# First layer of a two-layer metaformer: all eight images' scan blocks in one stream, the router as one stage behind them

## The chip, the cores and the metric

The kernel runs on one core of a Trainium2 chip. The metric is the device time of one execution in microseconds: 20141.26 us, the median of three runs (20123.66 to 20142.09). A core has five instruction queues that run in order and wait for each other through semaphores: PE (TensorE, matrix products into PSUM), DVE (VectorE), ACT (ScalarE), POOL (GpSimd) and SP (SyncE, which here issues the DMA transfers). Work is kept in order on each queue by the program; a queue whose first instruction waits holds everything behind it.

## The reference, cut to what matters

The net has two layers on an input of 8 images, 128 channels, 64 x 64 points (L = 4096). Only the first layer's mixer and the router of its mixture of experts are touched by the change.

```python
# layer 0, mixer: x = x + L0_conv(ln_c(x))
x_seq = x.reshape(b, c, L).swapaxes(1, 2); skip = x_seq
x_norm = (x_seq - mu) * rsqrt(var + 1e-5) * ln_g + ln_b
xp = x_norm @ in_w.T
x_tb = xp.reshape(b, h, w, D).swapaxes(1, 2).reshape(b, L, D)
U = stack([xp, flip(xp, 1), x_tb, flip(x_tb, 1)], 0)      # four directions
Y = vmap(_mamba)(U, ...)
...
out = skip_gate * (y_fused @ out_w.T) + (1.0 - skip_gate) * skip

def _mamba(u, ...):
    xh, z = split(u @ in_w.T, 2)
    xh = silu(conv1d(xh) + conv_b)                        # 4 taps
    dt, Bm, Cm = split(xh @ xproj_w.T, [R, R + N])        # N = 16 states
    dt = softplus(dt @ dt_w.T + dt_b)
    # h = exp(dt*A) * h + dt*x*B ;  y = sum_n h*C, along 4096 positions
    y = _selective_scan(xh, dt, A, Bm, Cm) + xh * Dp      # Dp is the "D term"
    return (y * silu(z)) @ out_w.T

# layer 0, experts: t = t + L0_ffn(ln_t(t))
probs = softmax(x @ gate_w.T + gate_b, axis=1)            # over the 4096 tokens, 64 experts
topv, topi = top_k of each expert, K = 8
pooled = einsum('bked,bke->bed', gathered tokens, topv)   # then the experts, then a scatter
```

## The kernel before, in words

Tensors lie as 128 channels on the partitions and positions along the free axis. `S` = 512 is a slice (8 slices an image), `CH` = 1024 a chunk of the scan; an image has 4 directions `d` of 4 chunks `j`, 16 chunks.

**A chunk's scan** works on 16 *slots*. 128 channels x 16 states are 2048 recurrences; a slot takes 128 of them (8 channels x 16 states). In slot n, in `scan_blocks`: PE spreads dt over the states into a PSUM tile `dA` (6 products in bf16, `expand`); ACT takes its exp; SP broadcasts 8 rows of `dtx_d` from DRAM to 128 partitions (`xE`, L621, 512 KB, four buffers); POOL multiplies it with B (`bx`, three buffers); DVE does the scan (L627) and the product with C (`hc`, L335), and keeps the last column (`last`, L347). PE then sums the states of four slots into the tile `y` by 8 products with `collect`. The code issues `xE` three slots ahead and `dA` and `bx` one slot ahead. On every engine the order is the order of the code: `ordered` ties each instruction to the one before it.

**A chunk's other steps** are put into slots by hand, in a table in `scan_steps`: each entry is a slot relative to the chunk's first. Slots -18 to -2, which lie in the chunk before, prepare the chunk: the four taps of the conv folded into `W_taps`, silu by tanh, dt by softplus, `dtx` (POOL, then a store to DRAM by SP, L526), B and C spread over the states, dt split into three bf16 parts. Slots 12 to 20 finish it: z product and its silu (`zs`), `skip` (DVE, L344: y + D x), `gate_y` (POOL: times zs, two halves), `out_product` (PE) and `out_add` (DVE: adds into `r`, the image's residual). ACT loads the tables of exp and ln at slot -11 and of exp and tanh at slot -4.

**Between two images** `run` closes the scan's pools and runs two generators in turns: `route_tokens` of the image just done and `scan_inputs` of the next. `route_tokens` stores `r` to `x1` in DRAM, takes the layer norm of each slice, the logits of 64 experts (on 64 partitions), turns the tokens over (`tk`), and then does the softmax over 4096 tokens, the eight largest (`MAX8`, `MATCH_REPLACE8`), and the pooled tokens (32 turns of P, 32 products). `scan_inputs` loads x, takes two norms one after the other (the outer `ln_c` and the mixer's own), projects into `xp`, copies the turned image `xt`, and writes `(1 - skip) x_norm + x` into `r`. After the last image only the router runs; then come the experts.

PSUM holds 8 banks: two `dA` tiles of two banks, `y` of two, and two banks `m`, which all other products of the scan stage share in turn.

Of the kernel before, what the change touches and what calls it, by code (L numbers as in the profile page):

```python
# [131 lines left out]
def layout(inputs):  # L132
# [46 lines left out]
    a.add("gate_b", i["L0_ffn_gate_b"])  # L179
# [99 lines left out]
class Net:  # L279
# [111 lines left out]
    def scan_weights(self, pool):  # L391
# [45 lines left out]
        self.wname, self.wt = "first", first  # L437

    def scan_steps(self, ch, xp, r, pl, ps):
# [76 lines left out]
        def dt(q):  # L516
            p = v[f"d{q}"]
            self.tt(p, v[f"sp_u{q}"], p, ALU.subtract)
            self.tt(make(f"dt{q}", 2), v[f"sp_r{q}"], p, ALU.add)
# [27 lines left out]
        def skip():  # L547
            self.stt(make("yt", 1, CH), ch["xs"], self.w(f"D{d}"), ch["y"], ALU.mult, ALU.add)

        def gate_y(q):  # L550
            yt = v["yt"][:, half[q]]
            self.tt(yt, yt, v["zs"][:, half[q]], ALU.mult, pool)

        def out_product(q):
            self.mm(bank(f"o{q}"), self.Wo[:, d, :], v["yt"][:, half[q]])

        def out_add(q):
            p, lo = v[f"o{q}"], CH * j + q * S
            lo = L - S - lo if back else lo
            if d < 2:  # L560
                to = r[:, lo : lo + S]
                to = to[:, ::-1] if back else to
            else:
                w0 = lo // 64
                to = r.rearrange("p (h w) -> p w h", w=64)[:, w0 : w0 + S // 64, :]
                to = to[:, ::-1, ::-1] if back else to
                p = p.rearrange("p (w h) -> p w h", h=64)
            self.tt(to, to, p, ALU.add)
# [10 lines left out]
            (-4, self.table, EXP_TANH_SET), (-3, part, 1, 1), (-3, rest, 1, 0), (-2, rest, 1, 1),  # L579
            (12, z_product, 0), (13, z_product, 1), (13, z_gate, 0), (14, z_gate, 1),  # L580
            (15, gated, v, "zs", 0), (16, gated, v, "zs", 1),
            (17, skip), (18, gate_y, 0), (19, gate_y, 1), (19, out_product, 0), (20, out_product, 1),
            (19, out_add, 0), (20, out_add, 1),
# [3 lines left out]
    def scan_blocks(self, xp, xt, r, pl, ps):  # L587
# [5 lines left out]
        chunks = [{"d": d, "j": j} for d in range(4) for j in range(NCH)]  # L593
        todo = {}
        for i, ch in enumerate(chunks):
            for at, step, *args in self.scan_steps(ch, xp if ch["d"] < 2 else xt, r, pl, ps):
                todo.setdefault(NQ * i + at, []).append((step, args))
# [5 lines left out]
        for n in range(min(todo), max(todo) + 1):  # L603
# [31 lines left out]
            if n % 4 < 2 and 4 <= n < total + 4:  # L635
# [4 lines left out]
                for g in range(4):  # L640
                    self.mm(ch["y"][32 * g : 32 * g + 32, h * S : (h + 1) * S], self.k("collect")[:, 32 * k : 32 * k + 32],
                            hcs[g0 + g][:, h * S : (h + 1) * S], start=k == 0, stop=k == 3)
# [5 lines left out]
        self.silus_done([])  # L648

# [7 lines left out]

    def scan_inputs(self, b, r, xp, xt, wk, ps):

        nc = self.nc  # L660
        made = [{} for _ in range(NS)]

        def bank(name):
            return ps.tile([C, S], F32, tag="b", bufs=4, name=name)

        def center(s):
            v = made[s]
            if s == 0:
                for t in (xp, xt):
                    nc.vector.memset(t[:, :PAD], 0.0)  # L670
                    nc.vector.memset(t[:, PAD + L :], 0.0)
            x = v["x"] = wk.tile([C, S], F32, name="x", bufs=4)
            nc.sync.dma_start(x, self.A["x"][b][:, s * S : (s + 1) * S])
            p = bank("ln_m")
            self.mm(p, self.k("mean"), x)
            v["xc"] = wk.tile([C, S], F32, name="xc", bufs=3)
            self.tt(v["xc"], x, p, ALU.subtract)
            v["sq"] = wk.tile([C, S], F32, name="xsq", bufs=3)
            self.act(v["sq"], v["xc"], AF.Square)

        def scales(s):
            v = made[s]
            p = bank("ln_v")
            self.mm(p, self.k("mean"), v["sq"])

            a, q = v["sq"], wk.tile([C, S], F32, name="xlq", bufs=3)
            self.act(a, p, AF.Ln, bias=self.k("e6"))
            self.act(q, a, AF.Exp, scale=-1.0)
            self.act(a, a, AF.Exp, scale=-0.5)
            self.tt(q, p, q, ALU.mult)  # L690
            self.tt(v["xc"], v["xc"], a, ALU.mult)
            self.stt(r[:, s * S : (s + 1) * S], v["xc"], self.unskip, v["x"], ALU.mult, ALU.add)
            v["q"] = q

        def second(s):
            v = made[s]
            self.rsqrt(v["q"], v["q"], self.k("e5"))
            self.tt(v["xc"], v["xc"], v["q"], ALU.mult, nc.gpsimd)
            self.ts(v["xc"], v["xc"], self.w("ln_g"), ALU.mult, self.w("ln_b"), ALU.add)

        def project(s):
            p = bank("xp_p")
            self.mm(p, self.w("in_w"), made[s]["xc"])
            xq = xp[:, PAD + s * S : PAD + (s + 1) * S]
            nc.scalar.copy(xq, p)
            nc.gpsimd.tensor_copy(
                xt[:, PAD : PAD + L].rearrange("p (w h) -> p h w", h=64)[:, s * 8 : s * 8 + 8, :],
                xq.rearrange("p (h w) -> p h w", w=64),
            )
            made[s] = None  # L710

        yield from self.pipeline(NS, (center, scales, second, project))

    def first_mixer(self, b, r, xp, xt):

        nc, tc = self.nc, self.tc
        with tc.tile_pool(name=f"scan{b}", bufs=1) as pl2, tc.tile_pool(name=f"scanps{b}", bufs=1, space=PSUM) as ps2:
            self.scan_blocks(xp, xt, r, pl2, ps2)

    def route_tokens(self, b, r, pl, wk, ps):  # L720

        nc = self.nc
        nblk = L // 128
        pr = pl.tile([NE, L], F32, name="pr")
        tk = pl.tile([128, nblk, C], F32, name="tk")
        ms = pl.tile([NE, NS], F32, name="ms")
        made = [{} for _ in range(NS)]

        def bank(name):
            return ps.tile([C, S], F32, tag="c", bufs=3, name=name)  # L730

        def center(s):
            v, sg = made[s], slice(s * S, (s + 1) * S)
            nc.sync.dma_start(self.x1[b][:, sg], r[:, sg])
            p = bank("ln_m")
            self.mm(p, self.k("mean"), r[:, sg])
            v["xc"] = wk.tile([C, S], F32, name="tn", bufs=3)
            self.tt(v["xc"], r[:, sg], p, ALU.subtract)
            v["sq"] = wk.tile([C, S], F32, name="tsq", bufs=3)
            self.act(v["sq"], v["xc"], AF.Square)  # L740

        def scale(s):
            v = made[s]
            p = bank("ln_v")
            self.mm(p, self.k("mean"), v["sq"])
            self.rsqrt(v["sq"], p, self.k("e5"))
            self.tt(v["xc"], v["xc"], v["sq"], ALU.mult)

        def logits(s):
            v, sg = made[s], slice(s * S, (s + 1) * S)  # L750
            p = bank("lg_p")
            self.mm(p[:NE], self.w("gate_w"), v["xc"])
            self.act(pr[:, sg], p[:NE], AF.Identity, bias=self.w("gate_b")[:NE])
            nc.vector.tensor_reduce(ms[:, s : s + 1], pr[:, sg], AX.X, ALU.max)
            p = bank("tp")
            for u in range(S // 128):
                nc.tensor.transpose(p[:, u * 128 : (u + 1) * 128], v["xc"][:, u * 128 : (u + 1) * 128], self.k("ident"))
            nc.scalar.copy(tk[:, s * 4 : s * 4 + 4, :].rearrange("p u c -> p (u c)"), p)
            made[s] = None

        yield from self.pipeline(NS, (center, scale, logits))
        m = pl.tile([NE, 1], F32, name="m")
        nc.vector.tensor_reduce(m, ms, AX.X, ALU.max)
        self.ts(m, m, -1.0, ALU.mult)
        sm = pl.tile([NE, 1], F32, name="sm")
        self.act(pr, pr, AF.Exp, bias=m, accum_out=sm)
        yield
        nc.vector.reciprocal(sm, sm)
        self.ts(pr, pr, sm, ALU.mult)
        m8 = pl.tile([NE, 8], F32, name="m8")  # L770
        nc.vector.max(m8, pr)
        yield
        P = pl.tile([NE, L], F32, name="P")
        nc.vector.match_replace(out=P, in_to_replace=m8, in_values=pr, imm_value=0.0)
        yield
        self.tt(P, pr, P, ALU.subtract)
        nc.sync.dma_start(self.P[b], P)
        yield
        pool = ps.tile([C, NE], F32, tag="pool", bufs=1, name="pool_p")
        PT = [None] * NS  # L780

        def turned(s):
            p = bank("Pt_p")
            for u in range(4):
# [897 lines left out]
    def run(self, ctx):  # L1682
# [13 lines left out]
        with tc.tile_pool(name="mid", bufs=1) as mp:  # L1696
            self.pooled = mp.tile([C, NE, nb], F32, name="pooled")
            with tc.tile_pool(name="l0", bufs=1) as pl:
# [3 lines left out]
                for b in range(nb + 1):  # L1702
                    with tc.tile_pool(name=f"in{b}", bufs=1) as rp, tc.tile_pool(name=f"inw{b}", bufs=2) as wk, \
                            tc.tile_pool(name=f"inps{b}", bufs=1, space=PSUM) as ps:
                        gens = []
                        if b:
                            gens.append(self.route_tokens(b - 1, r, rp, wk, ps))
# [43 lines left out]
```

## Time and profile before

| what | us |
|---|---|
| median of three runs | 20141.26 |
| the profiled execution, its own time | 20168.29 |
| its span, first to last instruction | 20166.5 |
| mean granted TensorE clock of the span | 0.942 of full speed |
| first scan starts | 130.5 |
| last scan ends | 9566.1 |
| spans of the eight images' scans, first start to last end | 1041.5, 1046.8, 1076.4, 1036.8, 1058.8, 1060.4, 1064.8, 1058.1 |
| last image's pooled tokens are copied, the experts begin | 9663.2 |

The rows of the profile read as follows. A group has the line of kernel.py, the engine, the operation, output <- input by tile names, shape, count, busy time and the mean length of one; behind it the idle time that the engine had just before, and what ended it. Many lines are those of helpers (L288 every matmul, L335 every tensor_tensor, L296 every activation), so a group is known by its tiles. A float32 matmul stands as two rows. In the first layer these are the instructions that the change and the prediction speak of:

| instruction | shape | count | mean us |
|---|---|---|---|
| scan, `dA<-dA,last,bx` (DVE, L627) | 128 x 1024 | 1536 | 2.350 |
| `hc<-dA,C` (DVE) | 128 x 1024 | 2048 | 1.224 |
| `bx<-xE,B` (POOL) | 128 x 1024 | 2048 | 2.354 |
| exp of `dA` (ACT) | 128 x 1024 | 2048 | 1.088 |
| skip, `yt<-xs,w_first,y` (DVE, L344) | 128 x 1024 | 128 | 1.272 |
| gate_y, `yt<-yt,zs` (POOL) | 128 x 512 | 256 | 1.268 |
| out_add, `r<-r,m` (DVE) | 128 x 512 | 256 | 0.675 to 1.305 |
| `MAX8`, `MATCH_REPLACE8`, `P<-pr,P` (DVE) | 64 x 4096 | 8 each | 4.42, 4.40, 4.42 |

### The profile page before, as it was taken

How to read it: one execution, taken by the hardware profiler on the slowest of the kernel's cores; microseconds unless marked ns; L12 is line 12 of the kernel's file. 1: busy time of each engine (PE TensorE's matmuls, PEld its weight loads, DVE VectorE, ACT ScalarE, POOL GpSimd, SP SyncE). 2: the span in 40 equal slices, each digit the busy share in tenths (PEclk: the TensorE clock that was granted, in tenths of full speed). 3: DMA queues.
4: the chain of work that ended last, by engine and by line, in shares of the span. 5: the costliest groups of instructions: out<-in, count | busy, mean ns of one | idle time of the engine just before them, and what ended most of it. 6: DMA issues, size and time to landing. Idle time of an engine off the chain costs nothing. (4 is left out here: it accounts for less than half of the span.)

```text
span 20166.5 us, 298179 instructions
## 1 busy us (share of the span) xinstructions
PE 16460.5 (82%) x113085; PEld 8450.3 (42%) x113085; DVE 15697.6 (78%) x20826; ACT 11182.7 (55%) x15819; POOL 9162.0 (45%) x6292
## 2 busy tenths in 40 slices
PE   6777777777777777777887889999999998998898
PEld 2222222222222222222644666666666666665343
DVE  7989899898998989899254677676767676776886
ACT  5555555555555555555253666666666666665553
POOL 6767677686767767577010222222222222221443
PEclk9989999899999999899686999999999999999899
DMA  4435354343544445444441001010001000001222
GB/s 115 139 109 136 108 133 133 110 140 107 135 116 125 136 109 133 107 138 127 134 129 53 27 27 28 26 28 26 28 26 28 26 28 26 27 27 32 81 99 78
DMA packets 814167, 1684.33 MB, mean 84 GB/s; under 512 B 180859, under 2 KB 413211, under 8 KB 803803
## 3 DMA queue, kind: packets, MB, share of 16 engines
q1 hardware_dynamic: 812734, 1665.25, 29.4%
q8 instruction: 896, 14.68, 0.3%
q14 instruction: 537, 4.40, 0.1%
HBM read 1440.67 MB, written 224.26 MB: 83 GB/s over the span
## 5 line engine op out<-in xcount | busy, mean ns | idle before, releaser
L335 POOL TENSOR_TENSOR bx<-xE,B 128x1024 f32<-128x1024 f32 x2048 | 4819.7, 2354 | 1471.4 <-DMA xE<-dtx_d 1347.8
L288 PE MATMUL dA<-parts,expand 128*128 128x512 bf16 x12288 | 3182.7, 397 | 2113.9 <-DVE last L347 1573.3
L296 ACT ACTIVATE dA<-dA,negA 128x1024 f32<-128x1024 f32 x2048 | 2228.6, 1088 | 3692.1 <-PE dA L288 3672.4
L627 DVE TENSOR_TENSOR_SCAN dA<-dA,last,bx 128x1024 f32<-128x1024 f32 x1536 | 3610.2, 2350 | 206.8 <-POOL bx L335 200.0
L288 PEld LDWEIGHTS <-expand 128*128 128x128 bf16 x12288 | 1072.0, 100 | 4822.3 <-DVE last L347 2751.8
L344 DVE SCALAR_TENSOR_TENSOR E_cm<-E_cm,gm_cm 128x1024 f32<-128x1024 f32 x2048 | 2423.9, 1224 | 410.9 <-ACT E_cm L296 410.5
L296 ACT ACTIVATE E_cm<-ss_p 128x1024 f32<-128x1024 f32 x2048 | 1977.0, 1030 | 1305.3 <-PE ss_p L288 1303.7
L335 DVE TENSOR_TENSOR hc<-dA,C 128x1024 f32<-128x1024 f32 x2048 | 2507.5, 1224 | 69.9
L1137 POOL COPY Sd_cm<-S_cm 64x128 f32<-64x128 f32 x1024 | 798.9, 780 | 2830.4 <-DVE S_cm L335 2697.1
L335 POOL TENSOR_TENSOR xD_cm<-tok_cm,D_cm 128x256 f32<-128x256 f32 x512 | 437.8, 855 | 2652.2 <-PE y_p L288 2526.8
L288 PE MATMUL y_p<-E_cm,pad_cm 128*32 128x128 f32 x32768 | 1324.3, 278 | 27.6 <-DVE E_cm L344 11.2
L627 DVE TENSOR_TENSOR_SCAN dA<-dA,bx 128x1024 f32<-128x1024 f32 x512 | 1173.2, 2291 | 181.6 <-POOL bx L335 180.8
L288 PE MATMUL ss_p<-ssB_cm,ssA_cm 128*128 128x512 bf16 x4096 | 1110.3, 384 | 215.3 <-ACT E_cm L296 197.2
L288 PE MATMUL y<-hc,kt 128*32 128x512 f32 x8192 | 1191.2, 646 | 28.5 <-DVE hc L335 28.5
L288 PEld LDWEIGHTS y_p<-E_cm,pad_cm 128*32 128x32 f32 x32768 | 905.8, 110 | 359.8 <-issue 185.9
L288 PE MATMUL bc_p<-stk_cm,W_cm 128*128 128x256 f32 x4096 | 1020.7, 392 | 21.4 <-DMA stk_cm<-xs 17.4
L335 DVE TENSOR_TENSOR gm_cm<-g_p,kt 128x1024 f32<-128x1024 f32 x512 | 624.2, 1219 | 346.4 <-PE g_p L288 336.7
L296 ACT ACTIVATE tok_cm<-tok_p 128x384 f32<-128x384 f32 x1024 | 502.2, 490 | 606.2 <-PE tok_p L288 450.8
L296 ACT ACTIVATE BC_cm<-bc_p 128x1024 f32<-128x1024 f32 x512 | 524.8, 1025 | 544.9 <-PE bc_p L288 540.4
L288 PEld LDWEIGHTS bc_p<-stk_cm,W_cm 128*128 128x128 f32 x4096 | 741.2, 191 | 192.6 <-issue 74.4
L288 PE MATMUL tok_p<-W_cm,stk_cm 128*128 128x200 f32 x4096 | 761.4, 339 | 0.0
L335 DVE TENSOR_TENSOR yy_cm<-yy_cm,y_p 128x256 f32<-128x256 f32 x496 | 207.7, 419 | 665.5 <-PE y_p L288 652.2
(394 smaller groups left out, 30674.4 us busy)
## 6 DMA issues: line engine op xcount, KB each, us to landing
xE<-dtx_d SPq DMA_DIRECT2D x2048, 512.0 KB
dtx_d<-dtx SPq DMA_DIRECT2D x256, 256.0 KB
pb<-p_d SPq DMA_DIRECT2D x64, 1024.0 KB
x<-x SPq DMA_DIRECT2D x192, 256.0 KB
ssA_cm<-cs_cm SPq DMA_DIRECT2D x3072, 4.0 KB
stk_cm<-xs SPq DMA_DIRECT2D x368, 128.0 KB
stk_cm<-y SPq DMA_DIRECT2D x368, 128.0 KB
x<-in_x_dram SPq DMA_DIRECT2D x64, 256.0 KB
```

Source lines behind the costliest of these rows:

```text
L288: self.ordered(self.nc.tensor.matmul(out, lhsT=lhsT, rhs=rhs, start=start, stop=stop))
L296: i = self.ordered(self.nc.scalar.activation(out, in_, func, **kw))
L335: self.ordered((eng or self.nc.vector).tensor_tensor(out, a, b, op))
L344: self.ordered(self.nc.vector.scalar_tensor_tensor(out=out, in0=a, scalar=s, in1=b, op0=op0, op1=op1))
L627: self.ordered(nc.vector.tensor_tensor_scan(out=t, data0=t, data1=bx.pop(n), initial=0.0 if ch["j"] == 0 else last[:, q : q + 1], op0=ALU. ...
L1137: nc.gpsimd.tensor_copy(Sd[gr, :, g * hi : (g + 1) * hi], S2[gr])
```

## The change

1. **One stream.** `scan_blocks` lists the chunks of all eight images, 128 of them, and the slots run through. The steps of the next image's first chunk lie in the last chunk of the image before, as for any other chunk. `first_layer` replaces `first_mixer`.
2. **Norms in slots.** `scan_inputs` goes. `input_steps` has the same work for one slice as a table of slots: the load at slot -6, three products at slots 1, 4 and 12 into the shared banks `m`, eight ACT operations, four POOL operations and the store of the residual (`r0`, new, in DRAM). The eight slices of the next image lie in chunks 7 to 14 of the current one; those of image 0 lie ahead of the stream, 12 slots apart. The mean is taken off by the product itself (`center` = identity - mean), and `ln_g`, `ln_b` are folded into `in_w`, `in_b`. No DVE operation is left in it.
3. **Image steps.** `image_steps` turns `xp` into `xt` (POOL, first six chunks), fetches `r0` and adds it into `r` (POOL, chunks 3 to 6), and stores `r` to `x1` behind the last chunk. Since `r` no longer starts with the residual, `out_add` of direction 0 is a copy on ACT.
4. **D term.** `skip` becomes 8 products on TensorE with a diagonal matrix into the open `y` (two halves of four); `gate_y` becomes one DVE product of `y` in PSUM and `zs`; both move by a slot, out_product and out_add go from 19 and 20 to 20 and 21.
5. **Router.** `route` runs after all scans, on pairs of images (64 + 64 experts on 128 partitions). It loads `x1` again, takes tokens and logits in one product (`W_route` = center beside center times gate_w, 192 columns, 128 tokens at a time), scales both with 1/std, and turns the logits. The pooling of one pair runs in turns with the logits of the next. The subtraction of P is on POOL, in four parts.

The diff, cut to its core:

```diff
         def dt(q):
             p = v[f"d{q}"]
             self.tt(p, v[f"sp_u{q}"], p, ALU.subtract)
-            self.tt(make(f"dt{q}", 2), v[f"sp_r{q}"], p, ALU.add)
+            v[f"dt{q}"] = v[f"sp_r{q}"]
+            self.tt(v[f"dt{q}"], v[f"dt{q}"], p, ALU.add)
...
-        def skip():
-            self.stt(make("yt", 1, CH), ch["xs"], self.w(f"D{d}"), ch["y"], ALU.mult, ALU.add)
-
-        def gate_y(q):
-            yt = v["yt"][:, half[q]]
-            self.tt(yt, yt, v["zs"][:, half[q]], ALU.mult, pool)
+        def diagonal():
+            t = self.D_diag = pl.tile([C, C], F32, name="D_diag", bufs=1)
+            self.ts(t, self.k("ident"), self.w(f"D{d}"), ALU.mult)
+
+        def skip(q):
+            for g in range(4):
+                rows_ = slice(32 * g, 32 * g + 32)
+                self.mm(ch["y"][rows_, half[q]], self.D_diag[:, rows_], ch["xs"][:, half[q]], start=False)
+
+        def gate_y():
+            self.tt(v["zs"], ch["y"], v["zs"], ALU.mult)
...
-            self.tt(to, to, p, ALU.add)
+            if d == 0:
+                self.ordered(nc.scalar.copy(to, p))
+            else:
+                self.tt(to, to, p, ALU.add)
...
-            (17, skip), (18, gate_y, 0), (19, gate_y, 1), (19, out_product, 0), (20, out_product, 1),
-            (19, out_add, 0), (20, out_add, 1),
+            (16, skip, 0), (17, skip, 1), (17, gate_y), (20, out_product, 0), (21, out_product, 1),
+            (20, out_add, 0), (21, out_add, 1),
...
+    def input_steps(self, b, s, xp, pl, ps):
...
+        def center():
+            p = bank()
+            self.mm(p, self.center, v["px"])
+            self.ordered(nc.scalar.copy(make("pxc", 1), p))
+            self.act(make("psq", 1), p, AF.Square)
...
+        def residual():
+            self.tt(v["px"], v["px"], v["var"], ALU.add, pool)
+            nc.sync.dma_start(self.r0[b][:, sg], v["px"])
...
+        return [(-6, load), (1, center), (4, variance), (6, log), (7, powers), (8, second_variance), (8, scaled),
+                (9, second_log), (9, unskipped), (10, second_power), (10, residual), (11, second_scaled), (12, project)]
...
+    def image_steps(self, b, r, xp, xt, pl):
...
+        for s in range(NS):
+            table += [(2 + 11 * s, turned, s), (62 + 5 * s, fetch, s), (66 + 5 * s, add, s), (262 + s, store, s)]
+        return table
...
-        chunks = [{"d": d, "j": j} for d in range(4) for j in range(NCH)]
+        chunks = [{"d": d, "j": j} for b in range(self.nb) for d in range(4) for j in range(NCH)]
+        per = NQ * 4 * NCH
...
+        for i, s in enumerate(range(NS)):
+            plan(-31 - 12 * (NS - 1 - i), self.input_steps(0, s, xp, pl, ps))
+        plan(-19, [(0, self.table, EXP_TANH_SET)])
+        for b in range(self.nb):
+            plan(per * b, self.image_steps(b, r, xp, xt, pl))
+            if b + 1 < self.nb:
+                for i, s in enumerate((2, 3, 4, 5, 6, 7, 0, 1)):
+                    plan(per * b + NQ * (7 + i), self.input_steps(b + 1, s, xp, pl, ps))
...
+    def route(self):
...
+                def products(n):
+                    q = ps.tile([128, 2, S], F32, tag="q", bufs=2, name="q")
+                    for u in range(NU):
+                        o = u % 2 * (C + NE)
+                        self.mm(q[:, u // 2, o : o + C + NE], made[n]["x"][:, u * 128 : (u + 1) * 128], routes)
...
+            for p in range(NPAIR + 1):
+                gens = []
+                if p:
+                    gens.append(pooled(p - 1, st[p - 1]))
+                if p < NPAIR:
+                    gens.append(logits(p, st[p]))
+                self.turns(*gens)
...
-                for b in range(nb + 1):
...
-                        self.turns(*gens)
-                    if b < nb:
-                        self.first_mixer(b, r, xp, xt)
+                with tc.tile_pool(name="l0s", bufs=1) as sp:
+                    self.first_layer(sp)
+                self.route()
             self.experts()
```

## The prediction

> **What bounds the kernel now.** I read the page first, then a table of busy time by stretch, then the waits inside the first layer, then the timeline of POOL at one chunk border. The page says that no engine is full over the span; the slices say why: in the first half DVE drops in eight places, and there DMA and POOL drop too.
>
> ```profile
> span 20166.5 us, 298179 instructions
> PE 16460.5 (82%) x113085; PEld 8450.3 (42%) x113085; DVE 15697.6 (78%) x20826; ACT 11182.7 (55%) x15819; POOL 9162.0 (45%) x6292
> DVE 7989899898998989899254677676767676776886
> ```
>
> The change touches only the first layer, 0 to 9663 us. Its stretches, columns as the profile gives them (busy us and instructions of PE, weight loads, DVE, ACT, POOL, then granted clock, DMA share, GB/s): head, scans of image 0, gap, scans of image 1, tail.
>
> ```profile
> 0.00:130.00 130.00, 68.87 (x108) 25.67 (x109) 42.40 (x94) 86.71 (x112) 31.05 (x29) 0.80 0.15 53
> 130.00:1172.00 1042.00, 783.07 (x3080) 248.64 (x3077) 1004.54 (x843) 577.77 (x742) 813.33 (x437) 0.97 0.49 136
> 1172.00:1315.00 143.00, 103.12 (x283) 47.74 (x284) 66.82 (x83) 79.07 (x135) 35.13 (x28) 0.76 0.16 48
> 1315.00:2362.00 1047.00, 783.59 (x3078) 249.40 (x3076) 1005.62 (x842) 578.06 (x742) 814.34 (x438) 0.96 0.50 135
> 9566.00:9663.00 97.00, 56.65 (x190) 30.43 (x190) 37.11 (x38) 33.64 (x52) 3.75 (x3) 0.73 0.27 83
> ```
>
> The reader is to see two things. In a scan stretch DVE is 96% busy and leads. In a gap nothing leads: no engine is above 72%, because router and norms of eight slices are chains of short steps. And the DMA share of a scan stretch stands at one half in every image. The waits from 130 to 9566 us tell why that half matters:
>
> ```profile
> POOL bx L335 <- DMA xE<-dtx_d: 1347.8, 1203, 5.0
> DVE dA L627 <- POOL bx L335: 380.8, 285, 13.1
> ```
>
> POOL waits for the broadcast xE in 1203 of 2048 slots, and what DVE waits for, it waits for through POOL. At the border of two chunks (POOL, start, length, idle before):
>
> ```profile
> 447.67 2.37 POOL L335 TENSOR_TENSOR bx<-xE,B 128x1024 f32<-128x1024 f32 x1 [1.07 <-DMA xE<-dtx_d]
> ...
> 454.28 2.35 POOL L335 TENSOR_TENSOR bx<-xE,B 128x1024 f32<-128x1024 f32 x1 [3.13 <-DMA xE<-dtx_d]
> ...
> 458.42 2.35 POOL L335 TENSOR_TENSOR bx<-xE,B 128x1024 f32<-128x1024 f32 x1 [0.54 <-DMA xE<-dtx_d]
> ...
> 462.74 2.35 POOL L335 TENSOR_TENSOR bx<-xE,B 128x1024 f32<-128x1024 f32 x1 [0.74 <-DMA xE<-dtx_d]
> ...
> 466.83 2.35 POOL L335 TENSOR_TENSOR bx<-xE,B 128x1024 f32<-128x1024 f32 x1 [0.52 <-DMA xE<-dtx_d]
> ...
> 470.78 2.35 POOL L335 TENSOR_TENSOR bx<-xE,B 128x1024 f32<-128x1024 f32 x1 [0.37 <-DMA xE<-dtx_d]
> ```
>
> xE lands every 4.1 us (458.42, 462.74, 466.83, 470.78), while a DVE slot without extras is scan 2.35 + hc 1.22 = 3.57 us. The transfer that goes out when the bx of 454.28 frees its buffer (456.63) is used at 470.78: a trip through the queue takes 14 us, three transfers ahead of it. And xE of a new chunk can't go out before dtx has landed, so the queue drains at each border: 6.6 us from 447.67 to 454.28. So in the scans DVE leads by a few per cent over the xE queue, and chunk by chunk one or the other sets the pace.
>
> The queue holds three waiting transfers and still the share is one half: eight of the 16 DMA engines carry xE, and they are never free. The Trainium skill, "DMA: Bandwidth & Descriptors", section "Why a DMA increments its semaphore by 16 and not by 1", says that a transfer runs on the largest number up to 16 that divides the slowest dimension of both sides; xE's source has 8 rows, hence 8 engines, the lowest-numbered ones. The share agrees.
>
> **The sum is made against the profiled execution, 20168.29 us (span 20166.5).** The median of the three runs, 20141.26, is 27 us lower; I take that off at the end.
>
> *Gaps, removed.* From the end of an image's last scan to the next image's first scan the trace has 143.5, 140.8, 142.1, 141.4, 142.7, 140.8 and 140.8 us, 992 together. In one stream the step costs what any slot border costs, the last hc of 1.22 us: 7 x 1.3 = 9. Gain 983.
>
> *Router, one stage behind.* Before, the last image's router ran alone: r done 9578.4, pooled copied 9663.2, 85 us. Now four pairs run there. PE per pair, from pitches in the trace: 64 products of 192 columns at 0.37 (tok_p of 200 columns: two rows of 0.186) = 24; 64 transposes at 0.17 = 11; 64 pool products at 0.45 (32 in 14.4 us per image) = 29; sum 64. DVE per pair: 16 x (0.67 + 0.69 + 0.42 + 0.33) = 34, and 2.35 + 4.42 + 4.40 for softmax, max and replace = 45. In order, each unit adds a step from DVE to ACT (Ln, Exp of 4 columns, 0.2 each) and back, 0.65: 10 more. So PE leads; with 8 us in which exp (3.7) and max hold the others, 72 a pair. First pair alone 55, three overlapped 216, last pooling alone 48 (softmax chain 16, four POOL subtractions 9.4, 22 of PE): 320. Bounds: 256 (PE alone, 4 x 64) and 412 (no overlap between pairs, 4 x (55 + 48)). Cost 320 - 85 = 235.
>
> *Head.* Before, the norms of image 0 took 77 us pipelined (17.6 to 95.1), then 35 us to the first scan at 130.5. Now each slice starts 12 slots behind the other, and without scans nothing overlaps: three products cold 2.05 each, ACT 0.59 + 0.63 + 0.59 + 0.62 + 0.62 + 0.68, POOL 4 x 1.27, hops 1.2 = 16.1 a slice, 129 for eight. 20.8 + 129 + 35 = 185. Cost 54; bounds 25 (12 us a slice) and 85 (20).
>
> *Scans.* Their spans sum to 8444 us. What the change does in them:
> - DVE loses the two out_adds of each d = 0 chunk (0.68 each, 64 of them: 43) and trades the skip (1.27) for gate_y (1.22; 6 in all). This counts only where DVE leads, I take 0.3: -15.
> - The first chunk of an image took 69.7 us, the others 66.2 on average, since its pipeline filled: 7 x 3.6 = -25.
> - Seven images get eight x loads and eight r0 stores in their chunks, and SP holds them between dtx and the next chunk's first xE: order xE, r0 store, second dtx, x load, xE. The r0 store makes SP wait for POOL's residual, which stands ahead of dtx on POOL (1.27). That is covered, as dtx lands behind xE anyway. The x load waits until an r0 store has landed, and with it xE, which all DVE work of the next chunk waits for. Bounds: 0 (all beside dtx's own trip) to 3.5 (two issues 0.7, two transfers of 1.0, a quarter of xE's 4.1, as 256 KB spread over twice the engines, and 0.8 of hops). I take 1.8, as load and issue are on the path and the store is not; 0.75 of it shows, since some borders have slack: 56 x 1.35 = 76.
> - Eight x1 stores go out in one bunch ahead of dtx in the next image's first chunk: 0 to 8 us, taken 6 x 0.75 x 7 = 32. Then 64 fetches of r0, 0 to 1.0 each, 0.5 taken: 31. ACT's copy into r in slot 20 waits for these stores; issued five slots (18 us) ahead against a trip of 14, I cost that at nothing; if they came later, the exp of the next slot would stand behind it.
> - The D term is 8 matmuls of the form of y (four take 1.06). In slot 16 PE has dA 1.47, y 1.06, D 1.06, a tap 0.5 = 4.1 against 3.57; in slot 17 dA, y, the norm's product 1.02, D: it ends 8.7 us after slot 16 began, and gate_y on DVE wants it at 7.15. A new DVE wait of 1.6 with inputs and 0.5 without, behind it the next scan: 56 x 1.6 + 72 x 0.5 = 126 if DVE leads everywhere, 0 if xE does; taken 57.
> - POOL loses gate_y (2 x 1.27) and gets four operations in an input chunk: 55 of 66 us, not leading. ACT gets 7 us in such a chunk, 46 of 66; no table load is added there.
>
> Together +155; bounds -330 (below) and +440. The sum: -983 + 235 + 54 + 155 = -539. 20168 - 539 = 19629, less 27: **19600**.
>
> By the page's rate of about 27 GiB/s per engine a 256 KB transfer over 16 engines is an estimate of 0.57 us, and the 232 new ones in the scans 131 us if all were on the path, against my 139 from the rows; no run here shows one alone.
>
> **Rivals.**
> - *All of it shows.* The queue leads nearly everywhere, every border pays 3.5 and nothing is absorbed: 196 + 56 + 64 + 126 = 442. For it: 1203 waits of POOL. Against: in many chunks DVE idles under 1 us. -983 + 235 + 54 + 442 = -252: 19889. The skill's rule on engines (same section) speaks for this one: loads over 128 partitions use the same eight engines as xE.
> - *Transfers are free and DVE leads alone.* Scans fall to DVE's busy time: 8 x (1004.5 - 6) + 126 = 8114, -330. -983 + 235 + 54 - 330 = -1024: 19117. For it: DVE is 96% busy. Against: POOL's waits for xE.
> - *Slower: SP's queue.* The x load waits for an r0 store that takes a whole further trip through the queue, 14 us, and every xE of the next chunk stands behind it: 56 x 14 = 784 on top of my sum, +245: 20386. It decides from 9.6 us a border (539 / 56). For it: SP works in order, and xE can't pass. Against: the store goes out just ahead of the second dtx, whose trip is waited for already.
>
> **How the numbers follow.** My sum 0.62 (own range 19400 to 19780); all shows 0.18; DVE alone 0.12; SP's queue 0.05; the rest, 0.03, a route or head beyond its bounds. The range of 8 in 10 cuts most of the outer two: 19260 to 19920. Faster by over 0.2% (40 us, about what a measurement of this kernel can tell from no change) 0.93, within 0.02, slower 0.05.
>
> **What would show.** Right: no stretch over 10 us between scans from the first to the last; first scan near 185, last near 8790; images near 1075 us a piece; about 320 us from r done to the experts' first product, PE the leader there; DVE waiting for PE's y at gate_y. Scan images of 1110 or more, with xE waits at each border, would be the first rival; below 1020 the second; SP waiting long on r0 stores the third. The prediction is wrong if the route takes over 412 us, or the images change by more than 60 us.

## The result, and the profile after

The changed kernel takes 19624.44 us (median of 4 runs, 19607.95 to 19633.83) against 20141.67 us before (4 runs, 20123.66 to 20153.9): a ratio of 0.9743, 95% interval 0.9726 to 0.976. 19600 was predicted. The sum came out; several of its terms did not, and by luck their errors made up for each other.

The page of the changed kernel, in its span, the line of engines and DVE's 40 slices:

```profile
span 19606.2 us, 301087 instructions
PE 16309.4 (83%) x113973; PEld 8446.2 (43%) x115013; DVE 15396.7 (79%) x20447; ACT 11171.1 (57%) x15902; POOL 9175.2 (47%) x6308
DVE  6999999999999999993555767677766676766886
```

The eight dips of DVE in the first half are gone; what is left is one slow stretch behind the scans. The first layer by stretch (head, all scans, router; columns as before the change):

```profile
0.00:166.70 166.70, 71.62 (x114) 25.82 (x116) 13.32 (x57) 74.38 (x114) 51.98 (x45) 0.75 0.17 57
166.70:8833.90 8667.20, 6800.32 (x26884) 2215.30 (x27392) 8110.09 (x6742) 5087.10 (x6742) 6717.35 (x3672) 0.95 0.51 139
8845.50:9120.60 275.10, 173.78 (x1286) 150.29 (x1286) 171.74 (x262) 119.96 (x265) 37.15 (x16) 0.86 0.34 100
```

DVE is 94% busy in the scans, so it leads there as before, and idles 557 us. What it and POOL wait for in that stretch:

```profile
POOL bx L335 <- DMA xE<-dtx_d: 667.9, 533, 4.5
...
DVE dA L757 <- POOL bx L335: 137.2, 135, 12.8
DVE zs L335 <- PE y L288: 135.4, 109, 2.3
DVE r L335 <- PE m L288: 115.3, 76, 2.6
...
DVE m L344 <- ACT sp_u L296: 71.8, 84, 1.2
```

POOL's waits for xE have halved (1347.8 before), and three waits stand in their place that the kernel before hardly had: gate_y for the D term, out_add for its product, and softplus (`m`) for ACT. One gate_y in a chunk with input work, DVE first and then PE:

```profile
4092.44 2.35 DVE L757 TENSOR_TENSOR_SCAN dA<-dA,last,bx 128x1024 f32<-128x1024 f32 x1
4094.82 1.23 DVE L335 TENSOR_TENSOR hc<-dA,C 128x1024 f32<-128x1024 f32 x1
...
4097.85 1.23 DVE L335 TENSOR_TENSOR zs<-y,zs 128x1024 f32<-128x1024 f32 x1 [1.74 <-PE y L288]
4098.99 2.35 DVE L757 TENSOR_TENSOR_SCAN dA<-dA,last,bx 128x1024 f32<-128x1024 f32 x1
```

```profile
4093.20 1.46 PE L288 MATMUL dA<-parts,expand 128*128 128x512 bf16 x6
4094.59 1.06 PE L288 MATMUL y<-hc,kt 128*32 128x512 f32 x8
4095.59 1.12 PE L288 MATMUL m<-px,center 128*128 128x512 f32 x2
4096.64 1.07 PE L288 MATMUL y<-xs,D_diag 128*32 128x512 f32 x8
```

PE has four things in that slot, and the one that DVE needs is last: the input step `center` stands ahead of the D term. The scan behind gate_y waits with it.

**Where the 560 us between the two profiled executions went** (20166.5 to 19606.2, spans). The gaps: -992. The scans themselves, from 8443.5 (the sum of eight images) to 8667.2: +223.7. The head, from 130.5 to 166.7: +36.2. The router, from r done to the pooled tokens copied, from 84.8 to 275.1: +190.3. Last scan to r done: -0.7. Everything behind the router, which the change does not touch, 10503.3 to 10485.6: -17.7. That last one is chance: in the twelve runs below the same stretch takes 10475 to 10503. The profile of the changed kernel is of its fastest run, that of before was 27 us above its median; so the profiles are 560 apart and the medians 517.

To split the +223.7, DVE's idle time was summed by slot from the trace's start and end of each DVE instruction. A slot here runs from the start of its scan to the start of the next scan, so the wait before a chunk's first scan is counted in slot 15 of the chunk before. Busy time grows by 60 (8049.8 to 8110.1), idle time by 163 (393.7 to 557.1). Mean idle of a slot in us, in the 56 chunks that carry input steps (chunks 7 to 14 of images 0 to 6) and in the other 72:

| slot, what waits there | before, 56 | after, 56 | before, 72 | after, 72 |
|---|---|---|---|---|
| 0, second scan of the chunk | 0.27 | 0.04 | 0.37 | 0.27 |
| 1, gate_y after the change | 0.10 | 1.83 | 0.15 | 0.55 |
| 4, first out_add after the change | 0.03 | 1.55 | 0.10 | 0.58 |
| 7, softplus | 0.05 | 0.95 | 0.07 | 0.13 |
| 15, first scan of the next chunk (bx for want of xE) | 1.13 | 0.03 | 1.35 | 0.87 |

So slots 1, 4 and 7 cost about 125, 120 and 55 us more, and the other slots, where most waits come from xE, give some 137 back, 46 of them in the first chunks of images.

### The profile page after: what moved, and what is told of

It reads as the page before. It is cut to its first block, busy times and chain, and to the rows that moved or that the text cites. A ratio compares the mean times of both kernels' runs of the same rounds, so it can differ in the third digit from the quotient of the medians.

```text
span 19606.2 us, 301087 instructions
## 1 busy us (share of the span) xinstructions
PE 16309.4 (83%) x113973; PEld 8446.2 (43%) x115013; DVE 15396.7 (79%) x20447; ACT 11171.1 (57%) x15902; POOL 9175.2 (47%) x6308
## 5 line engine op out<-in xcount | busy, mean ns | idle before, releaser
L288 PE MATMUL ss_p<-ssB_cm,ssA_cm 128*128 128x512 bf16 x3711 | 1067.4, 383 | 250.1 <-ACT E_cm L296 197.4
```

The source lines that it names most:

```text
L288: self.ordered(self.nc.tensor.matmul(out, lhsT=lhsT, rhs=rhs, start=start, stop=stop))
```

## The experiments

Theory 1 was read from that table: DVE leads, and what it now waits for is the order of work inside a slot; SP's queue costs nothing. Theory 2: the xE queue sets the pace, and waits for PE only take the place of waits for xE.

**Input steps behind the chunk's own.** The table of a slot lists the input steps first; here they are planned last.

```diff
         for b in range(self.nb):
             plan(per * b, self.image_steps(b, r, xp, xt, pl))
-            if b + 1 < self.nb:
-                for i, s in enumerate((2, 3, 4, 5, 6, 7, 0, 1)):
-                    plan(per * b + NQ * (7 + i), self.input_steps(b + 1, s, xp, pl, ps))
         for i, ch in enumerate(chunks):
             plan(NQ * i, self.scan_steps(ch, xp if ch["d"] < 2 else xt, r, pl, ps))
+        for b in range(self.nb - 1):
+            for i, s in enumerate((2, 3, 4, 5, 6, 7, 0, 1)):
+                plan(per * b + NQ * (7 + i), self.input_steps(b + 1, s, xp, pl, ps))
```

> Edit: in every slot the next image's input steps are issued behind the chunk's own steps, no longer ahead of them. Theory 1 (DVE sets the pace of the stream, and its new waits are for PE and ACT work that stands behind input work in the same slot): the waits in slots 1, 4 and 7 of the 56 chunks with input steps, 1.83, 1.55 and 0.95 us, fall to what the other chunks show, 0.55, 0.58 and 0.13; 56 x 3.07 = 172 less, of which up to 60 may come back as waits for xE: 19450 to 19515 us. Theory 2 (the xE queue sets the pace, DVE's waits for PE only take the place of waits for xE): no change, 19624 within 25, and the waits of POOL for xE rise again from 652 towards 1348.

Measured: 19512.01 us (19494.69 to 19515.76), ratio to before 0.968 (0.9663 to 0.9696); 112 less than the changed kernel. In the 56 chunks slots 1, 4 and 7 fall to 0.54, 0.98 and 0.39. But POOL's waits for xE rise:

```profile
POOL bx L335 <- DMA xE<-dtx_d: 995.4, 775, 5.1
...
DVE dA L757 <- POOL bx L335: 162.6, 177, 12.8
```

Both theories have a share: the order in a slot was a cost, and the xE queue takes a part of the gain.

**D term two slots earlier.** The `stop` flags that close the sums in `y` move with it; the diff leaves them out.

```diff
-            (16, skip, 0), (17, skip, 1), (17, gate_y), (20, out_product, 0), (21, out_product, 1),
+            (14, skip, 0), (15, skip, 1), (17, gate_y), (20, out_product, 0), (21, out_product, 1),
```

> Edit: the eight products of the D term go from slots 16 and 17 to slots 14 and 15, where PE has no products with collect. Theory 1: gate_y's wait, 1.83 us in 56 chunks and 0.55 in 72, falls to 0.1; 142 - 13 = 129 less, 19495, up to 40 more if xE takes some back. The prediction's step (57 of the 126 show): 19567. Theory 2: 19624 within 25.

Measured: 19549.82 us (19538.99 to 19581.05), 75 less, between the prediction's step and theory 1. gate_y's wait is gone (slot 1: 0.03 and 0.07). But slot 0 now idles 0.56 and 0.57, 51 us more over all chunks, most of it for ACT's exp, and POOL's waits for xE are 775.0:

```profile
DVE dA L757 <- ACT dA L296: 65.9, 133, 0.6
```

**Both.** The two diffs above together.

> Edit: both of the above. Theory 1: slot 1's wait goes in all chunks (129), slots 4 and 7 of the input chunks lose 0.97 and 0.82 (56 x 1.79 = 100): 19395, up to 90 more if xE takes some back. Theory 2: 19624 within 25.

Measured: 19538.53 us (19522.27 to 19545.0): 86 less where at least 139 was expected, and 27 more than the first edit alone. Its waits in the scans:

```profile
POOL bx L335 <- DMA xE<-dtx_d: 936.2, 735, 4.6
...
DVE dA L757 <- POOL bx L335: 187.6, 198, 12.8
...
DVE r L335 <- PE m L288: 72.1, 47, 1.7
DVE dA L757 <- ACT dA L296: 68.2, 155, 1.5
...
DVE zs L335 <- PE y L288: 1.7, 4, 0.7
```

gate_y's 135.4 went to 1.7; waits for POOL went from 137.2 to 187.6, and waits for ACT's exp from 19.8 to 68.2. So the forecast of theory 1 fails, but the queue is not alone in that: the new waits for ACT's exp (48 us) are nearly as large as the 53 us that are missing, and they come from the D term's new place. Whether the queue is a second leader close behind DVE is decided below, by the runs with 16 engines.

**Without r0's traffic.** To price what the prediction laid on SP's queue.

```diff
         def residual():
             self.tt(v["px"], v["px"], v["var"], ALU.add, pool)
-            nc.sync.dma_start(self.r0[b][:, sg], v["px"])
...
         def fetch(s):
-            v[s] = pl.tile([C, S], F32, name="px", bufs=2)
-            nc.sync.dma_start(v[s], self.r0[b][:, s * S : (s + 1) * S])
+            v[s] = xp[:, PAD + s * S : PAD + (s + 1) * S]
```

> Edit: the residual r0 is neither stored to DRAM nor fetched again (64 stores and 64 loads of 256 KB less); the x loads, and all operations of POOL, ACT and DVE stay, and what is added into r is xp in place of r0, so the output is not the reference's. The prediction's steps (x load behind the r0 store at the chunk border 76, fetches 31): 107 less, 19517. Theory 1 (the first slot of a chunk shows no wait of DVE, 0.04 us in the chunks with inputs, so SP's queue costs nothing there): 19624 within 20.

Measured: 19665.64 us (19628.3 to 19686.8), 41 more, with 34 MB of transfers less. Neither theory said so. The 41 us are at the edge of the noise: the ranges of the two kernels overlap (the changed kernel's goes up to 19633.83). The 107 us that the prediction's steps would give back did not come. In the profiled execution, the slowest of the four, POOL waits for xE much longer:

```profile
POOL bx L335 <- DMA xE<-dtx_d: 1147.9, 887, 4.5
...
DVE dA L755 <- POOL bx L335: 203.5, 197, 12.7
```

So r0's stores and loads are no cost on the path. Whether the kernel is slower without them is taken up below.

**D term back on DVE.**

```diff
-        def skip(q):
-            for g in range(4):
-                rows_ = slice(32 * g, 32 * g + 32)
-                self.mm(ch["y"][rows_, half[q]], self.D_diag[:, rows_], ch["xs"][:, half[q]], start=False)
+        def skip():
+            self.stt(ch["xs"], ch["xs"], self.w(f"D{d}"), ch["y"], ALU.mult, ALU.add)
...
-            (16, skip, 0), (17, skip, 1), (17, gate_y), (20, out_product, 0), (21, out_product, 1),
+            (17, skip), (18, gate_y, 0), (19, gate_y, 1), (20, out_product, 0), (21, out_product, 1),
```

> Edit: the D term goes back to DVE (one product of 1.27 us in slot 17, written over xs) and gate_y to POOL (two halves, slots 18 and 19); nothing else is undone. Theory 1 (on TensorE the D term cost DVE its wait for PE, 142 us, and the 32 diagonals, 36 us, and gave nothing back): DVE loses 36 + 142 and gains 6 + about 30 (it waits for y as before): up to 140 less, 19480 to 19560 if xE takes some back. Prediction's step (57 lost, 6 gained): 19570. If the D term on TensorE was a gain: above 19640.

Measured: 19498.78 us (19478.82 to 19524.21), ratio to before 0.9675 (0.966 to 0.9689), 126 less. Where the change put it, the D term on TensorE was a loss: slot 1 idles 0.03 and 0.11 without it, and DVE's busy time falls by 29.

**xE over 16 DMA engines.** The 128 rows of a slot are ordered state by state, so the source of the broadcast is 16 x 8 rows. The diff shows two of the places; `W_bc`, `A` and `collect` follow the same order.

```diff
-                nc.sync.dma_start(xE[u], bc(ch["dtx"][8 * q : 8 * q + 8, :], NST, 1))
+                nc.sync.dma_start(xE[u], bc(ch["dtx"][8 * q : 8 * q + 8, :], NST, 0))
...
-        self.expand = pool.tile([128, NQ * 8, NST], BF16, name="expand")
+        self.expand = pool.tile([128, NQ, NST, 8], BF16, name="expand")
```

> Edit: the 128 rows of a slot are ordered state by state (16 groups of 8 channels) and not channel by channel (8 groups of 16 states), so that the broadcast xE reads a source of 16 x 8 rows and not of 8 x 16; everything that depends on the order follows (expand, W_bc, A, collect). Bytes, transfers and instructions are the same. Theory A (xE is slow since it runs on 8 of 16 DMA engines, one transfer each 3.86 us while the queue is full): a transfer takes about half, POOL's waits for xE fall from 652 to under 200, and DVE loses the waits that come through POOL: 72 chunks without inputs x about 2.0 (slots 0, 2, 3, 5, 6, 15) = 144, and some 20 in the others: 19400 to 19520. Theory B (the memory or the 128 partitions set xE's pace, not the number of engines): 19624 within 25.

Measured: 19483.48 us (19473.33 to 19490.27), ratio to before 0.9666 (0.9652 to 0.9681), 141 less. The row "POOL bx <- DMA xE" is gone from the waits of the scans; the longest wait of bx and the two longest of DVE are now:

```profile
POOL bx L335 <- DVE dA L757: 492.4, 340, 4.4
...
DVE zs L335 <- PE y L288: 144.1, 127, 1.9
...
DVE r L335 <- PE m L288: 105.1, 68, 2.6
```

Slot 15 idles 0.03 in all chunks. From the trace's issue instructions and semaphore steps, the median time from the issue of an xE to its landing is 12.6 us before the change, 9.5 after, and 4.0 here. In the changed kernel the semaphore of an xE moves in nine steps, one 0.45 us after the issue and eight around the landing; here it moves in 16 steps, all around the landing. That bears out theory A. The Trainium skill's "DMA: Bandwidth & Descriptors", section "Why a DMA increments its semaphore by 16 and not by 1", gives the number of engines by the divisors of the slowest dimension; the trace agrees, with eight steps around the landing for 8 x 16 rows and 16 for 16 x 8.

**16 engines and both schedule edits.** The three diffs above together.

> Edit: that order of rows, input steps behind the chunk's own in each slot, and the D term in slots 14 and 15. Theory A with two leaders (DVE, and behind it the xE queue that took back 143 of the 229 which the two schedule edits should have given): with xE out of the way both show in full, DVE's idle time falls from 557 to some 150 (slots 4 and 7): 8110 + 150 = 8260 for the scans, 19220, 100 more at most. Theory B: as the two schedule edits alone, 19538 within 25.

Measured: 19336.01 us (19320.07 to 19351.88), 147 less than with 16 engines alone and 202 less than the schedule edits alone; the parts give 86 and 141, the two together 288. That is what two leaders look like: each hid part of what the other cost. DVE's idle time is 306, not 150: slot 0 idles 0.53 to 0.57, slot 4 1.01 and 0.42. DVE's longest wait is now the one for ACT's exp:

```profile
DVE dA L757 <- ACT dA L296: 99.9, 222, 0.6
```

**Diagonal on ACT.** 

```diff
-            self.ts(t, self.k("ident"), self.w(f"D{d}"), ALU.mult)
+            self.act(t, self.k("ident"), ID, scale=self.w(f"D{d}"))
```

> Edit: as the one before, and the diagonal matrix of the D term (32 of 1.12 us) is made by ACT in place of DVE. If DVE leads without gaps: 36 less than the one before. If another engine leads by then: no change.

Measured: 19322.24 us (19316.24 to 19329.58): 14 less, inside the two ranges. DVE's busy time falls by 20, so not all of the diagonals' 36 us was DVE's own work.

**The kernel before, with 16 engines and nothing else.** The diff of xE, with what follows from the order, in the kernel before.

> Edit: the kernel before, with the rows of a slot ordered state by state, so that xE runs on 16 engines; nothing of the change is in it. Theory A with two leaders in the kernel before (the prediction's opening: chunk by chunk DVE or the xE queue sets the pace): DVE's waits through POOL, 381 us in the scans, go, less about 100 that waits for PE and ACT take over: 19800 to 19900. If the queue bound nothing there: 20142 within 25. The rest of the change is then worth the difference to the changed kernel with the same edit (19483).

Measured: 19833.67 us (19821.93 to 19837.39), ratio 0.9835 (0.9819 to 0.9851): 320 below the runs of before beside it. The images' scans sum to 8132.7 us against 8443.5, and DVE's idle time in them falls from 394 to 112. Image 0:

```profile
129.50:1144.00 1014.50, 779.46 (x3022) 249.06 (x3077) 1001.15 (x842) 576.81 (x741) 810.83 (x436) 0.96 0.52 139
```

DVE is 99% busy. So the kernel before lost 311 us of scan time to the queue; the changed kernel loses only 124 (8667.2 to 8543.2), as its DVE waits for PE and ACT anyway. On top of 16 engines the change is worth 350 us (19833.67 to 19483.48), not 517.

**D term in slots 6 and 7.** The rest as with the diagonal on ACT.

```diff
-            *([(12, diagonal)] if j == 0 else []),
+            *([(3, diagonal)] if j == 0 else []),
...
-            (14, skip, 0), (15, skip, 1), (17, gate_y), (20, out_product, 0), (21, out_product, 1),
+            (6, skip, 0), (7, skip, 1), (17, gate_y), (20, out_product, 0), (21, out_product, 1),
```

> Edit: as the run with 16 engines, both schedule edits and the diagonal on ACT (19322), and the D term's products in slots 6 and 7 (the diagonal in slot 3) in place of 14 and 15. Theory (in slot 14 PE has dA, two taps and the D term, 4.9 us, so the exp that slot 0 of the next chunk needs comes 0.55 us late, in all 128 chunks): 0.5 x 128 = 64 less, 19258. If the wait belongs to something else: 19322 within 25.

Measured: 19161.72 us (19145.75 to 19168.44): 161 less, where 64 was expected. Slot 0 gave its 0.5 as expected; slot 4 fell too, from 1.03 and 0.38 to 0.72 and 0.33, and slots 7, 8 and 15 in the chunks with inputs from 1.03 together to 0.21. So PE probably ran late through more slots than the one that was looked at. The granted clock of the scans rose too, from 0.96 to 0.97, with PE's busy time down from 6772 to 6690 us; this run does not separate the two.

**out_product a slot earlier.**

```diff
-            (6, skip, 0), (7, skip, 1), (17, gate_y), (20, out_product, 0), (21, out_product, 1),
+            (6, skip, 0), (7, skip, 1), (17, gate_y), (19, out_product, 0), (20, out_product, 1),
```

> Edit: as the one before, and the two products of out_product in slots 19 and 20 in place of 20 and 21, out_add where it was. Theory (DVE's wait in slot 4, 1.03 us in the 56 chunks with inputs and 0.38 in the others, is for a product issued in the same slot): 85 less than the one before. Rival: out_product now holds a bank over a slot more, variance waits for it on PE and the next dA behind it: no gain, or up to 50 more.

Measured: 19068.27 us (19062.85 to 19077.85), ratio to before 0.9457 (0.9438 to 0.9476): 93 less again, the fastest of all. The granted clock is 0.99 by now, and its share of the 93 us is not known either. The rival's wait is there, but on PE only. All scans, and the two waits:

```profile
166.40:8284.60 8118.20, 6597.06 (x26908) 2130.11 (x27417) 8031.92 (x6710) 5099.41 (x6774) 6691.21 (x3671) 0.99 0.55 148
```

```profile
PEld m L288 <- DVE r L335: 105.6, 56, 2.1
...
DVE m L344 <- ACT sp_u L296: 3.7, 22, 0.2
```

DVE is 99% busy over 8118 us. The scans are now at the length of DVE's own work.

**Without r0, over 16 engines.** The two diffs together, in the changed kernel.

> Edit: the changed kernel without r0's stores and loads (xp is added into r in place of r0, so the output is not the reference's), with xE on 16 engines. The run without r0 alone was 41 us slower, not faster, and its POOL waited 1131 us for xE in place of 652. If that came through the xE queue: gone here, 19483 within 20, as the run with 16 engines alone. If it came from POOL, DVE or ACT: 41 more than that, 19524.

Measured: 19483.55 us (19473.84 to 19502.12), the same as with r0. So what there is of the 41 us came through the xE queue. In the run without r0 an xE that was issued at least 3 us before the landing of the one ahead landed 3.97 us after it, in the changed kernel 3.86, and this holds for 0.89 of the transfers in place of 0.82. That other transfers make the queue faster is not shown by this: by the same measure the kernel before, which has no r0, takes 3.87, and the other runs with r0 and eight engines 3.83 to 3.87. Why this one run has 3.97 is open.

## Why the prediction was right, point by point

- *The sum.* -539 was predicted against the profiled execution, -560 measured there, -517 between the medians.
- *Gaps, -983.* Right for the time: no two scans are more than 5.7 us apart. But the step said that only the last hc, 1.3 us, was left of a gap. The groups of DVE's scan work sum to 13 us less than before, while busy time inside the scans grew by 60. Most of that had been scan work that ran in the gaps, 64 us by the trace, 9.1 a gap: the last chunk's finish and the next first chunk's softplus. Some 11 us more come from neighbouring DVE instructions, which overlap less than before (324 us in place of 335). Moved work was counted as removed.
- *Router, +235.* +190. The first pair took 56.6 (55 predicted), a further pair 61.4 (72), the last pooling 34.3 (48). "So PE leads" was wrong. One pair, by stretch:

```profile
8902.10:8963.50 61.40, 43.15 (x321) 37.47 (x321) 42.51 (x66) 29.42 (x66) 9.29 (x4) 0.89 0.36 103
```

PE 43 and DVE 42.5 of 61.4: nobody leads. The pooling products were put at 0.45 us each from the pitch of the kernel before; here 16 of them take 1.97 to 3.41. What sets 61.4 was not tested. The waits point to the chain of a slice (product, square, sum, Ln, Exp, scale, turn) and to the 11 us of DVE's three long steps (softmax, max, replace), around which PE waits for `lgs` up to 10.2 us at a time.
- *Head, +54.* +36, within its bounds; the steps of two slices overlap a little (15.1 and 14.2 us between the first three slices, where 16.1 was taken).
- *DVE's operations, -15.* As groups -13, but from other parts: out_add -42 and gate_y for skip -6 in full, where 0.3 of them was taken, and the diagonals +36, which the step forgot.
- *First-chunk fill, -25.* About -46: idle time of a first chunk goes from 9.0 to 2.4 us in images 1 to 7.
- *Chain at the border, +76; x1 stores, +32; fetches of r0, +31.* All nothing, and with them the first rival's price, but for its 126 of gate_y. Before the first scan behind a chunk with inputs (slot 15 in the table) DVE idles 0.03 us, behind the others 0.87. SP does wait there, as the step said, but no engine that leads waits for SP:

```profile
SPq L751 <- DMA dtx_d<-dtx: 527.8, 139, 13.8
SPq L622 <- DMA r<-px: 193.3, 42, 9.7
```

The run without r0 shows the chain and the fetches to be no cost; the x1 stores were not taken out, but the first chunks, where they stand, idle less than the mean.
- *gate_y waiting for the D term, +57.* The wait per chunk was right (1.6 and 0.5 predicted, 1.83 and 0.55 measured); that xE would hide half of it was not: about 125 on the path, nearly the 126 that stood as the full price.
- *Not foreseen: out_add (+120) and softplus (+55).* The same cause one and two steps on: `variance` ahead of out_product on PE, `powers` ahead of softplus on ACT (input steps last: 0.98 and 0.39 in those slots; out_product a slot earlier: 0.03). For out_add this is a part only: in the chunks without inputs it waits 0.58 with no `variance` ahead of it. The step "POOL and ACT have time enough" looked at sums, not at who stands first in a slot.
- *Waits for xE, about -91 beside the first chunks.* Not in the sum at all: every wait of DVE elsewhere lets the queue catch up.

Against the sum, then, the scans lack 139 of costs that did not come, 91 that xE gave back and 21 of first chunks; they have 175 more for out_add and softplus, 68 for gate_y, 64 for busy time that was not seen (55 of work moved out of the gaps, beyond the 9 counted, the rest lost overlap) and 2 for DVE's operations: +58, of the 60 by which the measured 223.7 exceeds 155 + 9. The router was 45 too dear, the head 18, and the stretch behind them came out 18 shorter by chance. The total was right because errors of both signs met; that is luck, not the sum's merit.

The rivals: "all shows" named 1110 us an image; they took 1075 to 1093, and its mechanism, the border, was refuted; its price of the transfers fell with it, as r0's could be left out and gave nothing back. The estimate of 131 us by the rate in the Trainium skill's "DMA: Bandwidth & Descriptors", section "Specifications", shares that. The Trainium skill's rule on engines, section "Why a DMA increments its semaphore by 16 and not by 1" of the same page, by which the loads use the engines of xE too, did not make them a cost. "DVE leads alone" did not come about here, but its size, 330 us, is close to what 16 engines gave the kernel before (311). SP's queue stayed behind the work.

## What to carry to other kernels

Where two resources are a few per cent apart, taking one wait away shows little until the other goes too: price a pair of edits alone and together. When work is moved into slots of a fixed order, ask of each slot what the leading engine wants from it and whether the new work stands ahead of that; the sums of busy time do not tell it. And ask what of a removed stage was work of the stage that stays.

## What was not expected of the hardware

A broadcast of the same 512 KB landed 4.0 us after its issue with 16 x 8 source rows and 12.6 us with 8 x 16 in the kernel before, three waiting transfers included. Where the xE ahead had landed before the issue, it took 4.0 us (16 engines) against 6.0 (the changed kernel). The order of rows alone was worth 320 us to the kernel before. With the queue full, an xE on eight engines mostly took over 3.6 us (75% of them after the change), and 15% took under 3.0; what tells them apart was not found. Taking 34 MB of other transfers away made nothing faster: 41 us more, at the edge of the noise, with xE on eight engines, and no difference on 16. The granted clock in the scans was 0.95 in the changed kernel, 0.97 with the D term in slots 6 and 7, and 0.99 in the fastest; what raised it was not tested.
